# A decoder layer's self-attention: another opening, another written order of steps, another ending

## The chip, the cores and the metric

The kernel runs on one core of a Trainium2 chip. The metric is the device time of one execution in microseconds; lower is better. All numbers are float32.

A core has several engines, each with its own instruction queue that is worked in order: TensorE (PE, matrix multiplications; PEld is its loading of weights), VectorE (DVE), ScalarE (ACT), GpSimd (POOL) and SyncE (SP). SP here issues DMA transfers only. ACT issues a few as well, between its other work. Engines wait for each other by semaphores, so an instruction that waits also holds up everything written behind it on the same engine.

## The reference

A post-norm decoder layer of three parts, with a batch of 2 × 1024 tokens of 256 numbers:

```python
# 1: causal self-attention, 16 heads of 64, rotary positions
q = apply_rope(split_heads(x @ Wq)); k = apply_rope(split_heads(x @ Wk)); v = split_heads(x @ Wv)
sim = jnp.einsum('bid,bjd->bij', q, k) * scale
attn = softmax(where(causal, sim, -inf))
x = layernorm(x + merge_heads(attn @ v) @ Wo + bo)
# 2: cross-attention over 77 context tokens, 16 heads of 64
x = layernorm(x + xattn(x, ctx_1024))
# 3: a router takes the upper half of the tokens by score; they get a GELU network of 1024, the others keep x
x = layernorm(x + where(selected, ffn(x), x))
```

The change touches part 1 alone. Parts 2 and 3 come after it.

## The kernel before

The self-attention part works in 16 *pairs*: 2 batches times 8 pairs of heads (two heads of 64 fill 128 partitions). The class `Pair` holds one pair's tiles. Each pair goes through small *steps*, each named by a letter and up to two digits. The order in which the steps of several pairs are mixed is written by hand in three lists, and the block around them (`tc.manual_schedule()`) keeps it: on each engine instructions stand in the order in which the lists issue them.

- `opening` is a text of steps such as `1Pq0` (pair 1, step `Pq0`), from the first projections until the regular order takes over. `5=` stands for `fill(5)`.
- `steps` is the order inside one *period*, repeated for one pair after another. Each entry has an offset: in the period of pair n, `("w", 1)` is pair n+1's step and `("V0", -1)` that of pair n−1. A step that the opening has done already is passed over.
- `ending` is again a text, from pair 13's last output step on.

The steps, with their engine and the line that does the work:

| step | what it does | engine, line |
|---|---|---|
| Pk0, Pk1, Pq0, Pq1, Pv0, Pv4 | project half of the tokens to k, q or v, into a PSUM bank | PE L268, v L303 |
| Ek0 … Eq1; Ev0, Ev4 | copy that bank out, to `raw`; v to the tile `v` | ACT L276; v L312 |
| d0, d1 | swap the halves of `raw` into `turned`, for the rotation: two DMAs | SP L219 |
| c, s, a | rotate k and q: cosine, sine, sum | POOL L288, L291, L295 |
| w | spread: store the tile `v` to memory (`v_d`), 512 KB | SP L219 |
| l | copies: four DMAs read `v_d` back into `v4`, in four groups of 32 partitions | SP and ACT in turn, L322 |
| S0 … S4 | scores of a group of query tiles | PE L342 |
| T | least of the masked negated scores, by row | DVE L355 |
| X | exponentials, with their sums | ACT L363 |
| R | transpose 32 × 32 blocks of the exponentials | DVE L372 |
| V0 … V7 | output: exponentials times v4; V0 needs all of the pair's R | PE L410 |
| O0 … O3 | copy the output out | ACT L422 |
| Q, I, D, B | sums to a row, inverse, store, and load spread out over partitions (`over`) | PE L380, DVE, SP, SP |
| M, W | scale the output by `over`, store it | POOL L431, SP |
| L | load a pair's weights | SP |
| A, C, Y, Z; f, F, g, z | projection with Wo, sum and norm of one tile of 128 tokens, first and second batch (*closings*): load, project (L473), norm (two steps) | SP, PE, DVE |
| U | copy a closing's projection out of its bank | ACT |
| H, h | turn the second half of batch 0's x by PE, and copy it out | PE L202, ACT |

The tile `v` exists once: Ev0 of the next pair writes into it, and so it waits until the store w has read it. `v4` exists once, too: l waits for the V7 that reads it last. `turned` and `raw` exist twice, and the tiles of exponentials five times. Projections, outputs and a few others share a ring of four PSUM banks; scores have two of their own.

`fill(n)` (L240) runs n matmuls whose result nobody reads; the profile counts each of these as two (x8 for `fill(4)`). `pieces` (L228) says for each pair into how many more matmuls than the least its projections and scores are cut; `split` uses that up from one call to the next. The first DMA begun behind V1 and V7 is tied by `begin` (with `gate`) to those matmuls.

Before the opening the block loads x's first half, pair 0's weights, the rope tables and x's second half on SP, fills, turns the first half of x, fills again, and then follows the three lists.

Of the kernel before, what the change touches and what calls it, by code (L numbers as in the profile page):

```python
# [17 lines left out]
B, T, C = 2, 1024, 256  # L18
H, D = 16, 64
# [15 lines left out]
def decoder_layer(  # L35
# [24 lines left out]
    V, A, G, TE = nc.vector, nc.scalar, nc.gpsimd, nc.tensor  # L60
# [85 lines left out]
    with (  # L146
# [47 lines left out]
        def turn_x(b, first, last, pool=None):  # L194

            for i in range(first, last, 2):
                if i % NH == 0:
                    x_ts[b, i // NH] = e1.tile([P, NC, NB], F32, tag="xT", name=f"xT_{b}", bufs=3)
                pt = ring.tile([P, NC, 2, P], F32, tag="t", name="pt_x")
                for k in range(2):  # L200
                    for c in range(NC):
                        TE.transpose(pt[:, c, k, :], xs[b][:, i + k, c * P : (c + 1) * P], ident)  # L202
                keep = lambda pt=pt, i=i: A.copy(
                    x_ts[b, i // NH][:, :, i % NH * P : (i % NH + 2) * P], pt.rearrange("p c k q -> p c (k q)")
                )
                if b == 0 and i >= NH:
                    kept_later.append(keep)
                elif b == 0 and i == 0:
                    V.tensor_copy(x_ts[0, 0][:, :, : 2 * P], pt.rearrange("p c k q -> p c (k q)"))
                else:  # L210
                    keep()
# [13 lines left out]

        pieces = [0, 1, 13, 13, 11, 10, 11, 12, 13, 12, 8, 9, 8, 8, 9, 0]  # L228
        left = [pieces[0]]

        def split(first, last, most):
# [8 lines left out]
        def fill(n):  # L240

            t = ring.tile([P, NB], F32, tag="t", name="unread")
            for _ in range(n):
                TE.matmul(t, ident, ident.unsqueeze(1).to_broadcast([P, NB // P, P]), start=True, stop=True)  # L244
# [193 lines left out]
        class Closing:  # L438
# [46 lines left out]


        steps = [
            ("Eq0", 1), ("Ek0", 1), ("Ev4", 1), ("Eq1", 1), ("a0", 0), ("R40", -1), ("S0", 0), ("T00", 0), ("T01", 0),
            ("s1", 0), ("V0", -1), ("a1", 0), ("V1", -1), ("d0", 1), ("B", -2), ("S1", 0), ("V2", -1), ("T10", 0),
            ("V3", -1), ("V4", -1), ("T11", 0), ("S2", 0), ("X00", 0), ("V5", -1), ("R00", 0), ("X01", 0), ("R01", 0),  # L490
            ("c0", 1), ("Z", -15), ("X11", 0), ("T20", 0), ("V6", -1), ("T21", 0), ("V7", -1), ("w", 1), ("X10", 0),
            ("X20", 0), ("O1", -1), ("S3", 0), ("R10", 0), ("O0", -1), ("R11", 0), ("Q", -1), ("s0", 1), ("O3", -1),
            ("T31", 0), ("l", 0), ("C", 0), ("O2", -1), ("X31", 0), ("Pk1", 1), ("T30", 0), ("I", -1), ("Pv0", 2),
            ("X30", 0), ("M", -2), ("R20", 0), ("Ek1", 1), ("d1", 1), ("R31", 0), ("Ev0", 2), ("D", -1), ("S4", 0),
            ("R30", 0), ("Pq1", 2), ("L", 3), ("W", -2), ("A", 0), ("c1", 1), ("X21", 0), ("Pq0", 2), ("T41", 0),
            ("Pk0", 2), ("X41", 0), ("T40", 0), ("R21", 0), ("R41", 0), ("X40", 0), ("Pv4", 2),
        ]

        pairs = [Pair(n) for n in range(len(keys))]
# [23 lines left out]


        opening = """
            1L 0Pk0 0Ek0 0Pq0 0Eq0 0H 0h 0Pv0 0Pq1 0c0 0d0 0Pk1 0s0 0a0 0Pv4 0Eq1 0S0 0Ek1 0Ev0 1Pk1 0T00 0d1 0T01 1Pq1
            0c1 0Ev4 0s1 0X01 0X00 1Eq1 1Ek1 1Pv0 0a1 0S1 2L 0R00 0w 0R01 1d1 1Pv4 1c1 1Pq0 0T10 0T11 0S2 1Ev4 0T21 1Ev0
            0X10 1Eq0 1Pk0 1s1 1w 2Pq1 0T20 0R10 0l 1Ek0 1d0 0X11 0S3 2Pk0 0R11 0X21 0X20 0T30 1a1 0T31 0X30 0S4 1c0 3L
            0X31 1s0 0R20 0R30 0R21 1a0 2Eq1 0T41 0T40 2Pv4 2Pv0 0X40 2Ek0 0R31 0R40 2Pq0 2Ev4 5= 0X41 1S0 0R41 1T00
            2Eq0 2Ev0 0V0 0V1 1T01 2d0 0V2 1S1 1T11 0V3 1X00 0V4 0V5 1T10 1S2 1X01 1R00 1X11 0V6 0V7 2w 1X10 1T20 0O0  # L530
            1T21 1S3 1R10 1R01 0O1 1T31 2c0 1l 2Pk1 1X20 1R20 0O3 1T30 0O2 3Pv4 0Q 2Ek1 1S4 1X30 2s0 1X21 3Pq1 2c1 3Ev4
            1R11 3Pv0 2a0 3Pk0 1T41 2d1 1R30 1X31 3Pq0 2S0 1T40 1R21 0I 1X41 1X40 1R31 2s1 1R40 0D 1R41 2T00 3Ek0 3Eq1
            2a1 4L 3Eq0 3Ev0 1V0 1V1 3d0 2T01 2X00 1V2 2S1 1V3 1V4 2T10 2T11 1V5 0B 2R00 2S2 2X01 2T20 2T21 1V6 1V7 3c0
            2X11 2R01
        """


        ending = """
            14X10 12M 14X20 14S3 13O0 15s0 14X21 14R11 14R20 14l 13O1 14T31 14T30 14R21 14X30 14X31 15Pk1 15w 13Q 13I
            14S4 15Ek1 14T40 12W 4C 14T41 14X41 13O2 14R10 15a0 15d1 14R31 13O3 14R30 13D 14X40 15c1 14R40 14R41 15S0 4Y  # L540
            15T00 14V0 15T01 15X00 14V1 14V2 15X01 15s1 15a1 14V3 5A 13B 15R00 15S1 15T10 14V4 6A 15X10 14V5 15T11 15S2
            14V6 14V7 15X11 15R01 15T21 15l 15T20 13M 14O3 15S3 7A 15X20 5C 15X21 15R10 15T30 14O0 15T31 15R11 15X30
            15R21 14O1 15R30 15X31 13W 15S4 15R20 15T41 15T40 14Q 5U 14O2 15X41 14I 15R31 15X40 6C 15Q 2= 14D 15I 15R40
            6U 15R41 15V0 4Z 14B 5Y 15V1 15V2 0f 15V3 14M 1f 7C 15V4 15V5 5Z 6Y 15V6 6Z 15D 2f 15V7 15B 15O1 15O3 7U 0n
            15O2 15O0 0F 1F 2F 3f 1g 3F 2g 3g 7Y 4f 3z 0N 5f 7Z 4F 5F 1z 6f 6F 4g 0g 7f 2z 5g 5z 4z 6g 7F 7g 1N 6z 7z 0z
        """
        closings = [[Closing(b, i) for i in range(NT)] for b in range(B)]
        closing = {
# [6 lines left out]
        def do(n, step):  # L555
            if (n, step) in done or not 0 <= n < (NT if step in closing else len(keys)):
                return
            if step in closing:
                b, act = closing[step]
                act(closings[b][n])  # L560
            elif step == "H":
                turn_x(0, NH, NT)
            elif step == "h":
                for keep in kept_later:
                    keep()
            elif step == "N":
                load_cross(n)
            elif step == "n":
                turn_context()
            else:  # L570
                if n == last and step[0] == "O":
                    pairs[n].gathered_scaled(int(step[1]))
                elif n == 0 and step in ("c0", "s0", "a0"):
                    {"c": pairs[0].cosine, "s": pairs[0].sine, "a": pairs[0].rotated}[step[0]](0, V)
                else:
                    acts[step[0]](pairs[n], step[1:])

                if (n, step) in ((NP - 3, "S4"), (NP, "Pv0")):
                    turn_x(1, *((0, NH) if step == "S4" else (NH, NT)))
                if step == "V7" and n + 1 < len(keys):  # L580
                    left[0] = pieces[n + 1]
                if step == "W":
                    for f in later.get(n, ()):
                        f()
            done.add((n, step))
# [36 lines left out]
        with tc.manual_schedule():  # L622
            halves = x[0].rearrange("(t p) c -> p t c", p=P)
            nc.sync.dma_start(xs[0][:, :NH, :C], halves[:, :NH, :])
            do(0, "L")
            nc.sync.dma_start(cos[:, :NB], rope_cos[:, :NB])
            nc.sync.dma_start(xs[0][:, NH:, :C], halves[:, NH:, :])
            nc.sync.dma_start(sin[:, :NB], rope_sin[:, :NB])
            nc.sync.dma_start(cos[:, NB:], rope_cos[:, NB:])
            nc.sync.dma_start(sin[:, NB:], rope_sin[:, NB:])  # L630
            G.iota(xs[0][:, :, C], [[P, NT]], 0, 1, allow_small_or_imprecise_dtypes=True)
            fill(4)
            turn_x(0, 0, NH)
            fill(1)
            follow(opening)
            for period in range(-8, len(keys)):
                for step, further in steps:
                    if step == "A":
                        if period >= NP + 1:
                            do(period - NP - 1, "A")  # L640
                    elif step == "C":
                        for s in "CY":
                            do(period - NP - 2, s)
                    elif step == "Z":
                        do(period - NP - 3, "Z")
                    else:
                        do(period + further, step)
                    if (last - 2, "V7") in done:
                        break
                else:  # L650
                    continue
                break
            follow(ending)
# [10 lines left out]
    c1 = pool("cross1", 1)  # L664
# [91 lines left out]
    Q = HH // 2  # L756
# [396 lines left out]
```

## Time and profile before

| | us |
|---|---|
| median of three runs | 818.18 (814.99 to 819.43) |
| the profiled execution | 815.8, its span 814.0 |
| PE busy | 788.3 (97%) |
| DVE busy | 580.0 (71%) |
| POOL busy | 367.3 (45%) |
| ACT busy | 355.8 (44%) |
| first output matmuls (V0) of pairs 0, 1, 2, 3 | 55.85, 87.1, 117.3, 146.96 |
| V0 of pairs 9, 10, 11, 12, 13, 14 | 324.97, 358.8, 391.75, 424.33, 456.98, 482.8 |

Times count from the start of the span. In the rows of the profile, the first number is an instruction group's busy time (or its start, in a timeline or a chain), `L410` is a line of the kernel, `po_self<-pT,v` names what is written and what is read, and `x128` counts instructions. `[1.70 <-DVE neg L355]` says that the engine was idle for 1.70 us before the row, and that a result of DVE ended it. `SPq` and `ACTq` are DMAs issued by these engines; the duration of such a row is that of issuing, not of the transfer. `PEclk` is the granted clock of TensorE in tenths of full speed, slice by slice.

### The profile page before, as it was taken

To read this page: it belongs to the slowest core of one execution; us is meant where nothing else is said; L and a number is where in the kernel's file an instruction comes from. 1 tells how busy PE (TensorE), PEld (TensorE's weight loads), DVE (VectorE), ACT (ScalarE), POOL (GpSimd) and SP (SyncE) were. 2 spreads that over 40 slices of the span, in tenths; PEclk is the share of its full clock that TensorE was granted. 3 is DMA by queue.
4 is the path that set the end of the run, shared out by engine and by line. 5 is a ranking of instruction groups with operands and counts; after the bars stand their busy time and mean duration, and the time that the engine had idled before them with its cause. 6 is when DMAs were issued, how large, how long until landed. Compare 5 with 4: busy or idle time off the path is not lost.

```text
span 814.0 us, 26605 instructions
## 1 busy us (share of the span) xinstructions
PE 788.3 (97%) x11436; PEld 624.3 (77%) x11436; DVE 580.0 (71%) x1345; ACT 355.8 (44%) x842; POOL 367.3 (45%) x261
## 2 busy tenths in 40 slices
PE   9999999999999999999999989899999999999996
PEld 5566688888888888788888766688778888887745
DVE  2567779669669768678777797526577788888674
ACT  2555566556556655455554554101343333333130
POOL 1733554554554565375473553213032222262574
PEclk9999999999999999999999999999999999999998
DMA  4545387477477577567376466870450000011121
GB/s 168 181 101 144 106 230 207 155 210 200 144 195 209 163 210 203 168 171 208 123 203 180 136 184 159 236 258 1 160 193 1 1 1 0 1 46 58 55 103 52
DMA packets 65328, 112.32 MB, mean 138 GB/s; under 512 B 6497, under 2 KB 43707, under 8 KB 65211
## 3 DMA queue, kind: packets, MB, share of 16 engines
q1 hardware_dynamic: 59067, 89.64, 37.0%
q10 hardware_dynamic: 4608, 16.78, 7.9%
q0 software_dynamic: 1536, 4.20, 1.4%
q8 instruction: 90, 1.47, 0.8%
q14 instruction: 27, 0.22, 0.1%
HBM read 71.24 MB, written 22.59 MB: 115 GB/s over the span
## 4 chain that ended last, share of the span: by engine, by line
PE 87%; DVE 6%; issue 3%; POOL 3%; DMA 1%; ACT 0%; POOLq 0%; DVEq 0%; ACTq 0%
PE po_self L410 19%; PE ps_scores L342 17%; PE pp_kq L268 14%; PE pp_v L303 7%; PE po_cross L995 6%; PE ps_cross L943 6%; PE po_proj L473 6%; PE pp_h L886 3%; PE po_ffn L897 2%; DVE pT L372 1%; PE pt_p L975 1%; PE unread L244 1%; POOL comp L828 1%; POOL e L964 1%; PE ps_vo L739 1%
## 5 line engine op out<-in xcount | busy, mean ns | idle before, releaser
L363 ACT ACTIVATE p<-p,neg 128x768 f32<-128x768 f32 (+7 forms) x256 | 196.3, 768 | 166.2 <-DVE neg L355 163.9
L355 DVE CUSTOM_DVE_ANT_0 p<-ps_scores,fence 128x512 f32<-128x512 f32 (+7 forms) x256 | 179.6, 751 | 103.1 <-PE ps_scores L342 102.4
L372 DVE STREAM_TRANSPOSE pT<-p 128x512 f32<-128x512 f32 (+7 forms) x256 | 176.2, 740 | 11.5 <-ACT p L363 5.5
L410 PE MATMUL po_self<-pT,v 32*64 32x256 f32 (+6 forms) x7808 | 157.8, 297 | 11.9 <-issue 9.0
L410 PEld LDWEIGHTS po_self<-pT,v 32*64 32x64 f32 x7808 | 136.8, 131 | 37.3 <-issue 25.6
L342 PE MATMUL ps_scores<-kq 64*128 64x256 f32 (+3 forms) x1060 | 147.2, 411 | 0.0
L342 PEld LDWEIGHTS ps_scores<-kq 64*128 64x128 f32 x1060 | 93.2, 187 | 39.2 <-issue 26.5
L291 POOL TENSOR_TENSOR turned<-turned,sin 128x1024 f32<-128x1024 f32 x31 | 73.2, 2362 | 104.3 <-DMA turned<-raw 99.4
L268 PE MATMUL pp_kq<-xT,w_pair 128*128 128x256 f32 (+2 forms) x516 | 118.6, 382 | 0.0
L288 POOL TENSOR_TENSOR kq<-raw,cos 128x1024 f32<-128x1024 f32 x31 | 73.2, 2362 | 77.1 <-ACT raw L276 77.1
L268 PEld LDWEIGHTS pp_kq<-xT,w_pair 128*128 128x128 f32 x516 | 86.9, 191 | 24.1 <-issue 11.6
L964 POOL TENSOR_TENSOR e<-e,inv 128x616 f32<-128x616 f32 x32 | 38.2, 1216 | 113.0 <-DVE inv L963 67.3
L120 POOL TENSOR_TENSOR rs<-ve,neg_half 128x1 f32<-128x1 f32 x48 | 27.2, 570 | 108.6 <-DVE ve L118 107.4
L295 POOL TENSOR_TENSOR kq<-kq,turned 128x1024 f32<-128x1024 f32 x31 | 73.5, 2370 | 1.3
L995 PE MATMUL po_cross<-packed,pT 128*128 128x256 f32 (+1 forms) x320 | 72.5, 380 | 0.1
L943 PE MATMUL ps_cross<-wqk,x1T 128*128 128x308 f32 x256 | 69.2, 423 | 0.0
L995 PEld LDWEIGHTS po_cross<-packed,pT 128*128 128x128 f32 (+1 forms) x320 | 60.1, 190 | 9.4 <-ACT pT L981 0.3
L303 PEld LDWEIGHTS pp_v<-w_pair,xT 128*128 128x128 f32 x512 | 61.2, 192 | 4.0 <-issue 2.5
L303 PE MATMUL pp_v<-w_pair,xT 128*128 128x128 f32 x512 | 62.4, 276 | 0.0
L943 PEld LDWEIGHTS ps_cross<-wqk,x1T 128*128 128x128 f32 x256 | 47.4, 190 | 16.2 <-issue 0.8
L956 ACT ACTIVATE e<-e 128x616 f32<-128x616 f32 x32 | 22.9, 717 | 80.8 <-DVE e L952 80.8
L473 PE MATMUL po_proj<-wo,attnT 128*128 128x256 f32 x224 | 53.4, 391 | 1.2 <-issue 1.0
(128 smaller groups left out, 826.1 us busy)
## 6 DMA issues: line engine op xcount, KB each, us to landing
turned<-raw SPq DMA_DIRECT2D x64, 256.0 KB, 4.4
v<-v_d SPq DMA_DIRECT2D x32, 512.0 KB, 11.6
v<-v_d ACTq DMA_DIRECT2D x32, 512.0 KB, 7.3
v_d<-v SPq DMA_DIRECT2D x16, 512.0 KB, 4.6
over<-inv_d SPq DMA_DIRECT2D x32, 256.0 KB, 4.5
attn_d<-out_pair SPq DMA_DIRECT2D x14, 512.0 KB, 4.4
attnT<-attn_d SPq DMA_DIRECT2D x8, 512.0 KB, 5.2
vo_d<-vo SPq DMA_DIRECT2D x2, 1232.0 KB
```

The lines of the kernel that those rows point to most:

```text
L268: TE.matmul(pp[:, cols], self.w[:, c, "kq".index(of), :], x_ts[self.b, n][:, c, cols], start=(c == 0), stop=(c == NC - 1),)
L288: E.tensor_tensor(self.kq[:, :, n * NB : (n + 1) * NB], self.raw[n], self.twice(cos, n), ALU.mult)
L295: E.tensor_tensor(dst, dst, self.turned[n], ALU.add)
L303: TE.matmul(pv[:, i, :], x_ts[self.b, 2 * n // NT][:, c, toks], self.w[:, c, 2, :], start=(c == 0), stop=(c == NC - 1),)
L342: TE.matmul(self.ps[j][:, cols], self.kq[rows, 1, t * P : (t + 1) * P], self.kq[rows, 0, cols.start - at : cols.stop - at], start=True, st ...
L355: V.tensor_tensor_reduce(p[:, span], self.ps[j][:, span], fence[:, T - (t + 1) * P :], -SCALE, -MASKED, ALU.add, ALU.min, neg[:, i : i + 1],)
L363: A.activation(p[:, span], p[:, span], AF.Exp, bias=neg[:, i : i + 1], scale=-1.0, accum_out=self.sums[:, j, t : t + 1],)
L372: V.transpose(p_t[:, first : first + t * step + 1 : step, :], self.p[g, j][:, span].rearrange("p (n k) -> p n k", k=P),)
L410: ins = TE.matmul(self.po[r][j * D : (j + 1) * D, n:, :], self.v4[rows, NT * k + n, j * D : (j + 1) * D], p_t[rows, first:last:step, k * R ...
L473: TE.matmul(self.po, of, wo[:, c, :], start=(c == 0), stop=(c == NP - 1))
L943: TE.matmul(ps[:, g, : Q * S], self.x_t[:, c, :], wqk[:, c, self.b, h : h + Q, :].rearrange("p h s -> p (h s)"), start=(c == 0), stop=(c = ...
L995: TE.matmul(po, self.p_t[:w, k, :], packed[self.b][:w, k, :], start=(k == 0), stop=(k == NK - 1))
```

## The change

The numbers of fills, the pieces and the written order change; what each step does stays as it is.

- Fills: `fill(4)` in front of the first turning becomes `fill(2)`; the `fill(1)` behind it, `5=` in the opening and `2=` in the ending go.
- Opening: the turning of x's second half and `0Pq1` come ahead of `0Pv0`; `1d1` comes ahead of `0w`, and `1d0` ahead of `0l`; the others are mixed differently.
- Steps: on SP the order within a period was d0, B, w, l, d1, D, L, W, A and becomes B, d0, l, w, d1, W, A, L, D. On PE, V4 moves behind S2, and Pv4 ahead of Pk0. On ACT, l's share of the copies moves behind O1, O2, X20, O3 and O0, and the order of exponentials and copies changes a little, as does DVE's and POOL's.
- Ending: `15w` comes ahead of `14l`; closings and the second batch's loads are mixed differently.

```diff
-        pieces = [0, 1, 13, 13, 11, 10, 11, 12, 13, 12, 8, 9, 8, 8, 9, 0]
+        pieces = [2, 1, 13, 13, 11, 10, 11, 12, 13, 14, 8, 9, 8, 7, 5, 0]
...
         steps = [
-            ("Eq0", 1), ("Ek0", 1), ("Ev4", 1), ("Eq1", 1), ("a0", 0), ("R40", -1), ("S0", 0), ("T00", 0), ("T01", 0),
-            ("s1", 0), ("V0", -1), ("a1", 0), ("V1", -1), ("d0", 1), ("B", -2), ("S1", 0), ("V2", -1), ("T10", 0),
-            ("V3", -1), ("V4", -1), ("T11", 0), ("S2", 0), ("X00", 0), ("V5", -1), ("R00", 0), ("X01", 0), ("R01", 0),
-            ("c0", 1), ("Z", -15), ("X11", 0), ("T20", 0), ("V6", -1), ("T21", 0), ("V7", -1), ("w", 1), ("X10", 0),
-            ("X20", 0), ("O1", -1), ("S3", 0), ("R10", 0), ("O0", -1), ("R11", 0), ("Q", -1), ("s0", 1), ("O3", -1),
-            ("T31", 0), ("l", 0), ("C", 0), ("O2", -1), ("X31", 0), ("Pk1", 1), ("T30", 0), ("I", -1), ("Pv0", 2),
-            ("X30", 0), ("M", -2), ("R20", 0), ("Ek1", 1), ("d1", 1), ("R31", 0), ("Ev0", 2), ("D", -1), ("S4", 0),
-            ("R30", 0), ("Pq1", 2), ("L", 3), ("W", -2), ("A", 0), ("c1", 1), ("X21", 0), ("Pq0", 2), ("T41", 0),
-            ("Pk0", 2), ("X41", 0), ("T40", 0), ("R21", 0), ("R41", 0), ("X40", 0), ("Pv4", 2),
+            ("Eq1", 1), ("a0", 0), ("Eq0", 1), ("Ev4", 1), ("S0", 0), ("R40", -1), ("T00", 0), ("s1", 0), ("V0", -1),
+            ("T01", 0), ("Ek0", 1), ("a1", 0), ("V1", -1), ("S1", 0), ("B", -2), ("V2", -1), ("V3", -1), ("T10", 0),
+            ("T11", 0), ("S2", 0), ("X00", 0), ("R00", 0), ("X01", 0), ("V4", -1), ("X11", 0), ("c0", 1), ("V5", -1),
+            ("Z", -15), ("R01", 0), ("d0", 1), ("X10", 0), ("T20", 0), ("V6", -1), ("T21", 0), ("V7", -1), ("S3", 0),
+            ("R10", 0), ("Q", -1), ("O1", -1), ("R11", 0), ("O2", -1), ("X20", 0), ("O3", -1), ("s0", 1), ("O0", -1),
+            ("T31", 0), ("l", 0), ("X31", 0), ("C", 0), ("Pk1", 1), ("T30", 0), ("w", 1), ("Ek1", 1), ("X30", 0),
+            ("Pv0", 2), ("M", -2), ("Ev0", 2), ("S4", 0), ("d1", 1), ("W", -2), ("I", -1), ("R30", 0), ("R31", 0),
+            ("Pq1", 2), ("A", 0), ("Pq0", 2), ("X21", 0), ("T40", 0), ("T41", 0), ("Pv4", 2), ("L", 3), ("D", -1),
+            ("X40", 0), ("Pk0", 2), ("R21", 0), ("X41", 0), ("R41", 0), ("c1", 1), ("R20", 0),
         ]
...
         opening = """
-            1L 0Pk0 0Ek0 0Pq0 0Eq0 0H 0h 0Pv0 0Pq1 0c0 0d0 0Pk1 0s0 0a0 0Pv4 0Eq1 0S0 0Ek1 0Ev0 1Pk1 0T00 0d1 0T01 1Pq1
-            0c1 0Ev4 0s1 0X01 0X00 1Eq1 1Ek1 1Pv0 0a1 0S1 2L 0R00 0w 0R01 1d1 1Pv4 1c1 1Pq0 0T10 0T11 0S2 1Ev4 0T21 1Ev0
-            0X10 1Eq0 1Pk0 1s1 1w 2Pq1 0T20 0R10 0l 1Ek0 1d0 0X11 0S3 2Pk0 0R11 0X21 0X20 0T30 1a1 0T31 0X30 0S4 1c0 3L
-            0X31 1s0 0R20 0R30 0R21 1a0 2Eq1 0T41 0T40 2Pv4 2Pv0 0X40 2Ek0 0R31 0R40 2Pq0 2Ev4 5= 0X41 1S0 0R41 1T00
+            0Pk0 0Ek0 0Pq0 0Eq0 0H 0h 0Pq1 1L 0c0 0d0 0s0 0a0 0Pv0 0Pk1 0Ev0 0Pv4 0S0 0T01 0Eq1 1Pk1 1Pq1 0Ek1 0T00 1Eq1
+            0Ev4 0X00 0d1 0c1 0s1 0X01 1Ek1 0a1 1d1 0R00 1s1 1Pv0 0w 1Pv4 0R01 1c1 0S1 1Pq0 2L 1Eq0 1Pk0 0T10 0T11 0S2
+            0T21 1Ek0 0X11 0X10 1d0 0l 1Ev4 0T20 2Pq1 0R10 1Ev0 0S3 1w 0X21 0R11 1s0 0T31 1c0 0X20 2Pk0 0T30 0S4 0R20
+            2Ek0 0X30 2Eq1 0X31 0R30 1a1 0T40 0R21 1a0 2Pv4 0T41 3L 2Pv0 0X40 0X41 0R31 0R40 2Ev4 2Pq0 0R41 1S0 2Eq0
...
         ending = """
-            14X10 12M 14X20 14S3 13O0 15s0 14X21 14R11 14R20 14l 13O1 14T31 14T30 14R21 14X30 14X31 15Pk1 15w 13Q 13I
+            14S3 14X10 15s0 12M 15w 14X20 14X21 13O0 14R20 14R21 14T31 14T30 13O1 14l 13Q 15Pk1 14X31 14X30 14S4 13I
...
-            15R21 14O1 15R30 15X31 13W 15S4 15R20 15T41 15T40 14Q 5U 14O2 15X41 14I 15R31 15X40 6C 15Q 2= 14D 15I 15R40
-            6U 15R41 15V0 4Z 14B 5Y 15V1 15V2 0f 15V3 14M 1f 7C 15V4 15V5 5Z 6Y 15V6 6Z 15D 2f 15V7 15B 15O1 15O3 7U 0n
+            15R21 4Z 15R20 15R30 14O1 13W 15X31 15S4 15T41 14Q 15X41 15T40 6C 14I 15X40 15Q 15R31 5U 15R40 15I 14D 14O2
+            15R41 15V0 15V1 5Y 15V2 0f 15V3 7C 6U 1f 14B 15D 7U 15V4 5Z 15V5 14M 6Y 15V6 2f 15V7 15B 15O1 6Z 15O3 0n
...
-            fill(4)
+            fill(2)
             turn_x(0, 0, NH)
-            fill(1)
             follow(opening)
```

## The prediction

> **What bounds the kernel now.** First the page: engine totals and granted clock.
>
> ```profile
> PE 788.3 (97%) x11436; PEld 624.3 (77%) x11436; DVE 580.0 (71%) x1345; ACT 355.8 (44%) x842; POOL 367.3 (45%) x261
> ...
> PEclk9999999999999999999999999999999999999998
> ```
>
> TensorE (PE) is busy 97% of the 814.0 us span at full clock in every slice. Nothing else is near it, so the change can win only where PE stands (25.7 us in all) or runs matmuls nobody reads. It can lose wherever something new makes PE stand. So I read next, for one middle period, the chain of work that ended last.
>
> ```profile
> 295.65 3.42 PE po_self L410 x128
> ...
> 308.65 1.72 PE ps_scores L342 x16
> ...
> 323.23 1.73 PE ps_scores L342 x20
> 324.97 3.43 PE po_self L410 x128
> ```
>
> (Start, duration.) The chain is PE alone from one pair's first output matmuls (V0) to the next pair's. V7, the last, ends 13.0 us after V0. The eight periods from 87.1 to 324.97 take 237.87 us, 29.73 each. The four behind them hold a closing's projection (3.46 us): about 33 each.
>
> What stands close behind PE? The timelines of SP and ACT in that period:
>
> ```profile
> 308.71 0.34 SPq L219 DMA_DIRECT2D v_d<-v  x1
> 309.10 1.51 SPq L322 DMA_DIRECT2D v<-v_d  x2
> 314.30 1.14 SPq L219 DMA_DIRECT2D turned<-raw  x2
> ```
>
> ```profile
> 314.18 0.59 ACT L312 COPY v<-pp_v 128x512 f32<-128x512 f32 x1
> 314.66 0.94 ACT L363 ACTIVATE p<-p,neg 128x768 f32<-128x768 f32 x1
> ...
> 317.39 1.15 ACT L363 ACTIVATE p<-p,neg 128x1024 f32<-128x1024 f32 x1 [1.70 <-DVE neg L355]
> 318.59 1.15 ACT L363 ACTIVATE p<-p,neg 128x1024 f32<-128x1024 f32 x1
> ```
>
> The spread (step w, `v_d<-v`) is issued as V7 ends. Its landing is in the answer on DMA issues around 308.7:
>
> ```profile
> v_d<-v SPq DMA_DIRECT2D x1, 512.0 KB, 5.1
> ```
>
> So it lands at 313.8, and Ev0, which rewrites the single `v` tile, starts at 314.18: 0.4 us of slack. The two big copies v4 behind it take 12.2 us.
>
> **The change, part by part. (1) w behind the copies l, pairs 2 to 9.** SP's order in a period was d0, B, w, l, d1, D, L, W; it becomes B, d0, l, w, d1, W, A, L, D. Only w and l matter. What w costs behind l is shown by before's own ending, where 14l stands ahead of 15w:
>
> ```profile
> 470.34 1.24 SPq L322 DMA_DIRECT2D v<-v_d  x2
> 472.01 0.34 SPq L219 DMA_DIRECT2D v_d<-v  x1
> ```
>
> ```profile
> v_d<-v SPq DMA_DIRECT2D x1, 512.0 KB, 11.9
> ```
>
> There w lands 472.01 + 11.9 − 470.34 = 13.57 us after the first copy's issue. Call this time D. In the changed steps ACT's two copies stand behind O1, O2, X20, O3 and O0, and so start about 2.4 us later than SP's; at best w gains all of that: 11.2. I take the middle, 12.35.
>
> Ev0 now waits for w. Behind it on ACT, which works in order, stand X21, X40, X41; their results go through DVE's R41, R20, R40, and V0 needs all of them. Starts in the ACT lines give the pitch: Ev0 0.48, X21 1.03 (with the read of its sum), X40 1.20, X41 about 1.21. The last three transposes:
>
> ```profile
> 318.41 3.23 DVE L372 STREAM_TRANSPOSE pT<-p 128x768 f32<-128x768 f32 x3
> ```
>
> 0.48 + 1.03 + 1.20 + 1.21 + 3.23 = 7.15, and 0.15 for releases: 7.3. From V0 to the next V0: 13.0 + 0.1 + 12.35 + 7.3 = 32.75, against 29.73. PE, whose next Pk0 also waits for Ev0's bank, stands 3.0 us longer per period. Break-even is D = 8.9.
>
> The standing also costs clock. Around V0 of pair 14, by stretches (length, PE, PEld, DVE, ACT, POOL, clock, DMA share, GB/s):
>
> ```profile
> 480.58:483.99 3.41, 1.87 (x22) 1.20 (x18) 3.41 (x5) 0.82 (x2) 0.00 (x0) 1.00 0.99 362
> 483.99:487.40 3.41, 3.19 (x64) 2.17 (x72) 3.26 (x16) 1.73 (x7) 1.50 (x2) 0.50 0.31 123
> 494.22:497.63 3.41, 2.05 (x99) 1.54 (x87) 3.05 (x11) 2.93 (x8) 0.90 (x1) 1.00 0.78 181
> ```
>
> A stretch with 1.87 us of PE work was followed by one at half clock; one with 2.05 was not followed by a drop. The price is in PE's timeline, pair 14's outputs against pair 15's:
>
> ```profile
> 484.21 7.42 PE L410 MATMUL po_self<-pT,v 32*64 32x256 f32 x250 [0.59 <-DVE y L483]
> ...
> 515.62 5.86 PE L410 MATMUL po_self<-pT,v 32*64 32x256 f32 x248 [0.28 <-DVE pT L372]
> ```
>
> 7.42 − 5.86 = 1.56 us. A gap of 3.0 us leaves some 3.41 us stretch with at most 3.41 − 1.5 = 1.91 of work, even split in the middle. The Trainium skill ("TensorE: Matmul & The Clock Gate", Part 1) drops to half rate only after an idle window of about 3.4 us, so by it a 3.0 us gap is free: period 32.75. By the row it is 34.3. I take the row: this chip dropped on a partly idle stretch. Eight periods: 8 × 34.3 − 237.9 = **+36.5** (by the rule +24).
>
> **(2) The same order in pairs 10 to 13.** PE's own period is 32.6 to 33.8 there, no shorter than 32.75, and the wait is covered by the projection: +1, with 0 and +6 as bounds. The copies of x's second batch, queued on ACT behind the wait, add 0.5. Together **+1.5**.
>
> **(3) Opening.** Before, V0 of pair 0 is at 55.85:
>
> ```profile
> 1.45 6.00 PE L244 MATMUL unread<-ident 128*128 128x512 f32 x8 [1.45 <-POOL ident masks.py:199]
> ...
> 49.75 4.46 PE L244 MATMUL unread<-ident 128*128 128x512 f32 x10
> 54.13 1.78 PE L342 MATMUL ps_scores<-kq 64*128 64x512 f32 x12
> ```
>
> With two fills instead of four, four passes stay of eight: the first took 1.02, the next 0.85 each (half clock), so PE is free at 1.45 + 1.02 + 3 × 0.85 = 5.0; the DMA of x's first half landed at 4.71. The transposes run 5.0 to 6.4; Pk0 starts at 6.9 instead of 9.03. Then H waits for x's second half (10.78) and Pq1 for its copies, which returns about 0.8. From there to S1 POOL's rope bounds (S1 27.73, now about 28.4), so the lead is used up and S4 still ends near 44. But before, PE filled from 49.75 because 1S0 waited for 1a0 (ended 52.94), whose swap was queued behind v's copies (landed 47.4). The changed order has that swap ahead. V0 then follows pair 0's last transpose, 7.1 to 7.8 after S4: about 51. That is −4.9; I take **−4.5**, bounds −7.5 (S4 earlier by its 2 us lead) and 0 (copies v4, now issued at 37, landing late). The Skill (same page, Part 4) says that transposes don't count as PE work for the clock. Then removing fills leaves the stretch 2.7 to 6.1 too idle, and the clock opens at 9.5, +1.3. The row has no such case: fills filled that stretch. I give no charge, as the half before 5.0 is still filled, and keep +1.3 in the range.
>
> **(4) Ending.** 15w goes ahead of 14l, which is the good order, but v4 of pair 14 then lands at about 470.3 + 0.4 + 12.2 = 482.9, where its V0 stands (482.77): even. Without the `2=` fill (1.88 us at 512.18, in a wait that remains) PE stands about 2.7 us before 15V0, and the same half-clock stretch follows: **+1.5**, bounds 0 and +4.
>
> **(5) At nothing.** V4 behind S2 and Pv4 before Pk0 swap places on a PE that has both ready. The pieces' sum goes from 138 to 137: one matmul. SP's d1 lands behind w, about 28 us after V0 (27.6 before); s1 and a1 on POOL (2.4 us each) still end by 33, and S1 wants them at V0' + 3.4, 36. If that cover were gone it would cost its lateness, under 2 us a period. D, L and W have over half a period each. The cross and router stages behind 561 are untouched.
>
> Sum on the profiled span: 814.0 + 36.5 + 1.5 − 4.5 + 1.5 = 849.0. The median of the runs, 818.18, stands 4.2 above that span (the profiled run itself 815.8, so 1.8 of it lies around the span and 2.4 between the runs): **853**.
>
> **The rivals.** *The stall without the clock (R2):* the page's rule holds. 849.0 − 12.5 + 4.2 = 841. For it: 1.87 and 2.05 are close, and pair 14's slow stretch is one case. *The copies worse (R4):* D is 13.6 in every period, and the C periods show it: 8 × 1.25 + 5 more = 868. For it: 13.57 is the only row. *Hidden (R3, the other side):* SP's copies run faster alone and w lands within 8.9 us of the first copy's issue. Then no period grows, the ending has its fill's place covered, and only the opening is left: 814.0 − 4.5 + 4.2 = 813.7, 0.55% faster. For it: w alone needs 5.1 us and ACT's half comes later. Against: the order is one queue's, and every row has w plus copies at 12 us or more. It decides at D = 8.9.
>
> **How the numbers follow.** A measurement of this kernel tells about 0.5%, 4.1 us. Chances: forecast 0.50, R2 0.22, R4 0.15, R3 0.13. R3 lies across the bound: 0.08 faster, 0.05 same. All others are slower: 0.87. Range: low, R2 with D at 11.2 (8 × 31.6 − 237.9 = +15) and the good opening: 814.0 + 15 + 1.5 − 7.5 + 4.2, about 828; high, R4 with the ending at +4 and the opening at −3.5: 872. That leaves R3 and little else out.
>
> **What would show it.** Right: ACT's group `v L312` waits for DMA `v_d<-v`, 6 to 8 us a period; `po_self L410` waits for DVE `pT L372` about 3 us in each of eight periods; V0 to V0 is 34 in pairs 2 to 9 and 33 in 10 to 13; the granted clock is below 9 in slices of the first 40%; V0 of pair 0 is near 51. Wrong: w lands within 9 us of the first copy, or Ev0 finds its tile free, or PE stands under 1.5 us a period (no clock drop).

## The result, and the profile after

The changed kernel takes 872.6 us (median of 4 runs, 864.7 to 873.4) against 818.8 before (814.99 to 821.11): a ratio of 1.064 (95% interval 1.061 to 1.068). The forecast was 853, with a range up to 872. The direction and the place are right. The size is at the upper edge: 54 us more instead of 35, as a time 0.6 us beyond the range's end, as a ratio (1.064 against 872 / 818.18 = 1.066) just within it.

The page of the changed kernel, engine totals and granted clock, and from its groups PE's output matmuls and ACT's copies of v:

```profile
PE 802.7 (92%) x11412; PEld 640.7 (74%) x11412; DVE 581.3 (67%) x1345; ACT 349.6 (40%) x842; POOL 366.7 (42%) x261
...
PEclk9989999999899999999999999999999999999988
...
L410 PE MATMUL po_self<-pT,v 32*64 32x256 f32 (+6 forms) x7808 | 168.2, 305 | 34.3 <-issue 30.2
...
L312 ACT COPY v<-pp_v 128x512 f32<-128x512 f32 x32 | 18.7, 589 | 86.3 <-DMA v_d<-v 81.2
```

The same group of copies before:

```profile
L312 ACT COPY v<-pp_v 128x512 f32<-128x512 f32 x32 | 18.7, 586 | 18.4 <-PE pp_v L303 15.1 <-issue 3.2
```

The span is 871.6 us, 57.6 longer. PE stood 43.2 us longer, and it was busy 14.4 us longer, although 9.6 us of fills are gone: it ran more stretches at half clock (mean granted clock 0.975, before 0.992). The copies of v waited 81.2 us for the DMA that reads their tile, in 12 waits. Before, this group stood 18.4 us in all, and none of it for that DMA.

V0 to V0, before and after, shows where the time came from:

| | before | after | difference | forecast |
|---|---|---|---|---|
| start to V0 of pair 1 (opening) | 87.1 | 91.5 | +4.4 | −4.5 |
| pair 1 to 9, eight periods | 237.8 | 283.9 | +46.1 | +36.5 |
| pair 9 to 13, four with a projection | 132.0 | 137.7 | +5.7 | +1.5 |
| pair 13 to 15 (ending) | 57.6 | 56.5 | −1.1 | +1.5, with the next row |
| from V0 of pair 15 | 299.5 | 302.1 | +2.5 | |

One period of the changed kernel, pair 5 to 6. First SP's timeline, then the DMA answer on the spread, then ACT's timeline:

```profile
249.14 1.04 SPq L322 DMA_DIRECT2D v<-v_d  x2
250.23 0.49 SPq L219 DMA_DIRECT2D v_d<-v  x1
```

```profile
v_d<-v SPq DMA_DIRECT2D x1, 512.0 KB, 12.4
```

```profile
249.28 0.31 ACTq L322 DMA_DIRECT2D v<-v_d  x1
249.39 0.95 ACT L363 ACTIVATE p<-p,neg 128x768 f32<-128x768 f32 x1
...
250.32 0.65 ACT L422 COPY out_pair<-po_self 128x256 f32<-128x256 f32 x2
...
262.67 0.59 ACT L312 COPY v<-pp_v 128x512 f32<-128x512 f32 x1 [6.52 <-DMA v_d<-v]
263.16 0.94 ACT L363 ACTIVATE p<-p,neg 128x768 f32<-128x768 f32 x1
...
264.09 1.14 ACT L363 ACTIVATE p<-p,neg 128x1024 f32<-128x1024 f32 x1
...
265.22 1.14 ACT L363 ACTIVATE p<-p,neg 128x1024 f32<-128x1024 f32 x1
```

V7 ends at 249.11, and V0 of pair 6 starts at 269.81. The spread, which before landed 5.1 us after V7, is issued behind SP's two copies and lands at 262.65. Ev0 starts there, 13.5 us after the first copy. The three exponentials behind it follow without a gap, and then DVE:

```profile
266.48 3.23 DVE L372 STREAM_TRANSPOSE pT<-p 128x1024 f32<-128x1024 f32 x3 [1.28 <-ACT p L363]
```

These are R41, R20 and R40. PE then starts V0 after 2.8 us of standing, besides 0.5 us ahead of Pk0. This is the forecast's chain, link by link.

The opening did not go as forecast. Here is the chain that ended last, up to V0 of pair 0, and one row of ACT:

```profile
35.07 9.70 DMA turned<-raw
...
44.92 2.36 POOL turned L291
47.29 2.30 POOL kq L288
49.59 4.64 POOL kq L295 x2
...
54.27 3.36 PE ps_scores L342 x12
57.63 4.54 PE po_self L410 x113
```

```profile
49.62 0.59 ACT L276 COPY raw<-pp_kq 128x512 f32<-128x512 f32 x1 [6.74 <-POOL kq L288]
```

PE was early up to here: S4 starts at 40.92 (42.09 before). The swap 1d0 was issued at 34.6 instead of 37.5, and its second half landed at 44.8 instead of 47.4. But POOL now does 1c0 and both 1a1 and 1a0 behind 1s0, which waits for that landing. Four instructions of 2.3 to 2.4 us end at 54.2, where two had ended at 52.9. And ACT's 2Eq1 stands 6.74 us, because 1c0 still reads the tile that it writes; pair 0's last exponentials are queued behind it.

### The profile page after: what moved, and what is told of

It is laid out like the page before. It is cut to its first block, busy times and chain, and to the rows that moved or that the text cites. A ratio compares the mean times of both kernels' runs of the same rounds, so it can differ in the third digit from the quotient of the medians.

```text
span 871.6 us, 26584 instructions
## 1 busy us (share of the span) xinstructions
PE 802.7 (92%) x11412; PEld 640.7 (74%) x11412; DVE 581.3 (67%) x1345; ACT 349.6 (40%) x842; POOL 366.7 (42%) x261
## 3 DMA queue, kind: packets, MB, share of 16 engines
q10 hardware_dynamic: 4608, 16.78, 8.8%
## 4 chain that ended last, share of the span: by engine, by line
PE 65%; DMA 14%; ACT 6%; issue 5%; DVE 4%; POOL 4%; SPq 1%; POOLq 0%; ACTq 0%; DVEq 0%
PE po_self L410 17%; PE ps_scores L342 12%; DMA turned<-raw 8%; PE po_cross L994 6%; PE ps_cross L942 6%; PE pp_kq L268 6%; PE po_proj L473 6%; ACT p L363 3%; PE pp_h L885 3%; PE pp_v L303 3%; DMA attn_d<-out_pair 2%; ACT raw L276 2%; PE po_ffn L896 2%; DMA v_d<-v 1%; PE pt_p L974 1%
## 5 line engine op out<-in xcount | busy, mean ns | idle before, releaser
L372 DVE STREAM_TRANSPOSE pT<-p 128x768 f32<-128x768 f32 (+7 forms) x256 | 179.1, 748 | 87.2 <-ACT p L363 81.2
L410 PE MATMUL po_self<-pT,v 32*64 32x256 f32 (+6 forms) x7808 | 168.2, 305 | 34.3 <-issue 30.2
L410 PEld LDWEIGHTS po_self<-pT,v 32*64 32x64 f32 x7808 | 149.2, 135 | 57.3 <-issue 48.9
L342 PE MATMUL ps_scores<-kq 64*128 64x256 f32 (+3 forms) x1052 | 152.8, 418 | 5.1 <-POOL kq L295 5.1
L268 PE MATMUL pp_kq<-xT,w_pair 128*128 128x256 f32 (+2 forms) x520 | 123.1, 385 | 15.1 <-ACT v L312 13.9
L342 PEld LDWEIGHTS ps_scores<-kq 64*128 64x128 f32 x1052 | 99.4, 189 | 46.9 <-issue 28.4
L288 POOL TENSOR_TENSOR kq<-raw,cos 128x1024 f32<-128x1024 f32 x31 | 73.2, 2362 | 73.8 <-ACT raw L276 73.8
L295 POOL TENSOR_TENSOR kq<-kq,turned 128x1024 f32<-128x1024 f32 x31 | 73.2, 2363 | 1.3
L942 PEld LDWEIGHTS ps_cross<-wqk,x1T 128*128 128x128 f32 x256 | 47.4, 190 | 16.2 <-issue 0.7
L312 ACT COPY v<-pp_v 128x512 f32<-128x512 f32 x32 | 18.7, 589 | 86.3 <-DMA v_d<-v 81.2
```

Of the source, the lines that this page charges most:

```text
L268: TE.matmul(pp[:, cols], self.w[:, c, "kq".index(of), :], x_ts[self.b, n][:, c, cols], start=(c == 0), stop=(c == NC - 1),)
L288: E.tensor_tensor(self.kq[:, :, n * NB : (n + 1) * NB], self.raw[n], self.twice(cos, n), ALU.mult)
L295: E.tensor_tensor(dst, dst, self.turned[n], ALU.add)
L342: TE.matmul(self.ps[j][:, cols], self.kq[rows, 1, t * P : (t + 1) * P], self.kq[rows, 0, cols.start - at : cols.stop - at], start=True, st ...
L372: V.transpose(p_t[:, first : first + t * step + 1 : step, :], self.p[g, j][:, span].rearrange("p (n k) -> p n k", k=P),)
L410: ins = TE.matmul(self.po[r][j * D : (j + 1) * D, n:, :], self.v4[rows, NT * k + n, j * D : (j + 1) * D], p_t[rows, first:last:step, k * R ...
```

## The experiments

**1. w in front again.** In the changed kernel:

```diff
-            ("Z", -15), ... ("V7", -1), ("S3", 0),
+            ("Z", -15), ... ("V7", -1), ("w", 1), ("S3", 0),
...
-            ("T31", 0), ... ("T30", 0), ("w", 1), ("Ek1", 1), ("X30", 0),
+            ("T31", 0), ... ("T30", 0), ("Ek1", 1), ("X30", 0),
```

> The changed kernel with one entry of the steps moved: the spread w stands directly behind V7 again, so on SP ahead of the copies l; all else as changed. Theory (w's place behind l makes Ev0 late): the standing in pairs 1 to 9 (+46.1 in the two traces) and in the four periods with a projection (+5.7) goes, V0 to V0 is again 29.5 to 30 in pairs 2 to 9, and the time is 872.6 - 52 = about 820 (817 to 824). Rival (the other moves of the steps carry it: ACT's order, B ahead of d0, Pv4 ahead of Pk0): still above 850.

Measured: 822.4 us, ratio to the kernel before 1.003 (0.999 to 1.008). Pair 1 to 9 took 240.9 us. The group of v's copies, with nothing left of the wait:

```profile
L312 ACT COPY v<-pp_v 128x512 f32<-128x512 f32 x32 | 18.7, 587 | 6.2 <-PE pp_v L303 6.2
```

One entry of a list takes back 50 of the 54 us. The kernel before with the changed opening alone takes 824.3 us (experiment 6), so no cost of the other moves of steps and ending is seen beyond the noise once w is in time.

**2. w behind, alone.** In the kernel before:

```diff
-            ... ("V7", -1), ("w", 1), ("X10", 0),
+            ... ("V7", -1), ("X10", 0),
...
-            ("T31", 0), ("l", 0), ... ("Pk1", 1), ("T30", 0), ("I", -1), ("Pv0", 2),
+            ("T31", 0), ("l", 0), ... ("Pk1", 1), ("T30", 0), ("w", 1), ("I", -1), ("Pv0", 2),
```

> The kernel before with one entry of the steps moved: w goes behind l, to the place between T30 and Ek1 that it has in the changed list; opening, ending, fills and all other steps as before. Theory: nearly the whole loss of the steps by this alone, 818.8 + 46 + 6 = about 870 (860 to 875), w landing 13.5 us after the first copy's issue. Rival (the loss needs the changed order of ACT or SP as well): under 840.

Measured: 845.7 us, ratio 1.028 (1.021 to 1.036). Both expectations missed. From pair 1 to 9 w landed 13.2 to 13.6 us after the first copy, as in the changed kernel, but from Ev0 to V0 it took 5.15 us in place of 7.14. Pair 1 to 9 took 266.0 us (+28), and the four projection periods 133.3 (+1.3). So something else of the changed steps makes the late w dearer, though no cost of it is seen by itself.

**3. The changed kernel with the end of its period put back.**

```diff
-            ... ("w", 1), ("Ek1", 1), ("X30", 0),
+            ... ("w", 1), ("Ek1", 1), ("X30", 0), ("R20", 0),
...
-            ... ("X21", 0), ("T40", 0), ("T41", 0), ("Pv4", 2), ("L", 3), ("D", -1),
-            ("X40", 0), ("Pk0", 2), ("R21", 0), ("X41", 0), ("R41", 0), ("c1", 1), ("R20", 0),
+            ... ("X21", 0), ("T41", 0), ("T40", 0), ("Pv4", 2), ("L", 3), ("D", -1),
+            ("X41", 0), ("Pk0", 2), ("R21", 0), ("X40", 0), ("R41", 0), ("c1", 1),
```

> The changed kernel with w still behind l, and only the end of the period put back into the order of before: R20 directly behind X30, T41 ahead of T40, X41 ahead of X40. Behind the late Ev0 stand then X21, X41, X40 and R40, with R21 and R41 beside them: 5.15 us from Ev0 to V0 as in the run with w alone moved, instead of 7.14. Theory (two parts that multiply: w late, and a longer tail behind it): 2.0 us less in each of the eight periods and about 1.2 less in the four with a projection, so 872.6 - 16 - 5 = about 851 (846 to 856), near the run with w alone moved (845.65). Rival (the rest of that difference comes from clock or from SP's order): above 860.

Measured: 849.3 us, ratio 1.038 (1.034 to 1.042), pair 1 to 9 266.1 us. ACT's and DVE's timelines behind the late Ev0:

```profile
255.87 0.59 ACT L312 COPY v<-pp_v 128x512 f32<-128x512 f32 x1 [6.54 <-DMA v_d<-v]
256.35 0.94 ACT L363 ACTIVATE p<-p,neg 128x768 f32<-128x768 f32 x1
257.28 1.14 ACT L363 ACTIVATE p<-p,neg 128x1024 f32<-128x1024 f32 x1
258.41 1.14 ACT L363 ACTIVATE p<-p,neg 128x1024 f32<-128x1024 f32 x1
```

```profile
258.54 2.38 DVE L372 STREAM_TRANSPOSE pT<-p 128x1024 f32<-128x1024 f32 x2 [0.15 <-ACT p L363]
```

Ev0 is as late as before, but R41 runs beside X40, and only R40 is left behind it: V0 at 261.02, 5.15 us after Ev0. In the changed order R41 waits for the last exponential, and R20, ready long before, stands behind it on DVE: two transposes more in series. This order shows no cost while Ev0 has slack (experiment 1); behind a late Ev0 it is worth 872.6 − 849.3 = 23 us.

**4. All copies l on ACT's queue**, in the changed kernel. This was meant to tell the place in a queue from the load on the transfer engines.

```diff
-                    (nc.scalar, nc.sync)[r % 2].dma_start(
+                    nc.scalar.dma_start(
```

> The changed kernel with all four copies l issued by ACT, none by SP; the list is unchanged, so w is still written behind l, but is the first of SP's queue after V7. Theory A (w is late since it stands behind copies in its own queue): w lands 5 to 7 us after V7, Ev0 finds its tile free, and the time falls to about 822 (816 to 828) as with w written first. Theory B (the copies take the transfer engines, whichever queue they stand in): w lands 10 us or more after V7 and the time stays above 855. In both, v4 lands about 13 us after V7, early enough.

Measured: 826.9 us, ratio 1.013 (1.008 to 1.018): the time that theory A expected. But the run does not tell the theories apart. SP's and ACT's timelines of one period:

```profile
225.68 0.34 SPq L219 DMA_DIRECT2D v_d<-v  x1
230.27 1.12 SPq L219 DMA_DIRECT2D turned<-raw  x2
```

```profile
225.82 0.31 ACTq L322 DMA_DIRECT2D v<-v_d  x1
226.18 1.06 ACTq L322 DMA_DIRECT2D v<-v_d  x1
227.27 1.00 ACTq L322 DMA_DIRECT2D v<-v_d  x2
```

With no copy ahead of it on SP, w was issued 0.14 us before the first copy, and not behind the copies. It landed 4.0 us after its issue (3.9 after the first copy) in the periods where its landing is seen, and v's copies stood for PE only (6.0 us in all). v4 landed about 14.5 us after the first copy, early enough. So w came first both in its queue and in time.

What was issued behind the copies shows the load. The swap d1 (`turned<-raw`) was issued at 230.27, 4.6 us after w, on a queue that held no copy. Issues and landings, as medians in us, come first for d1 here, then for d1 in the changed kernel, where two copies and w stand ahead of it in its own queue (253.73), and then for d0 there, with no copies under way (240.28):

```profile
turned<-raw SPq DMA_DIRECT2D x2, 256.0 KB, 9.8
```

```profile
turned<-raw SPq DMA_DIRECT2D x2, 256.0 KB, 9.5
```

```profile
turned<-raw SPq DMA_DIRECT2D x2, 256.0 KB, 4.7
```

The copies delay d1 by about 5 us, whichever queue they stand in. In the queue rows from 231 to 235 the transfer engines work for q10 alone, which is ACT's (its bytes went from 16.78 to 33.56 MB with this edit):

```profile
q10 hardware_dynamic: 228, 0.85, 103.1%
```

And in this kernel's opening pair 1's w was issued at 38.79, behind two swaps of its own queue and 2.8 us after the last of four copies on ACT's:

```profile
v_d<-v SPq DMA_DIRECT2D x1, 512.0 KB, 10.8
```

The changed kernel's w at that place took 11.4 us. So what is shown is that w has to be issued before the copies. That a queue of its own would help it behind them is not shown, and the load on the engines counts.

**5. Fills in the gap.** In the changed kernel, ahead of V0 of pairs 2 to 9:

```diff
-            ... ("S0", 0), ("R40", -1), ("T00", 0),
+            ... ("S0", 0), ("K", -1), ("R40", -1), ("T00", 0),
...
+            if step == "K":
+                if 2 <= n <= 9:
+                    fill(2)
```

> The changed kernel with two unread matmuls (1.7 us of PE at full clock) put between S0 and V0 in pairs 2 to 9, where PE stands 2.8 us; nothing else changed. Theory (the half-clock stretches come from that standing): the drops at 197, 306 and, if the gap behind Ev0 counts, 224 go, and the time is 872.6 - 4 to 7 = about 867 (863 to 870). Rival (clock drops do not depend on it, or the fills push V0): 872 or more.

Measured: 883.2 us, ratio 1.080 (1.075 to 1.085). Pair 1 to 9 took 279.9 us instead of 283.9: the half-clock stretches at 197 and 306 are gone, that at 220, behind Ev0, is not. That part went as expected. But the four periods with a projection, of which only the first has a fill at its start, took 149.7 instead of 137.7 us: PE stood 1.8 to 2.9 us in each, in V5 to V7, without a wait that the profile shows, and each time a half-clock stretch followed. Every such standing ends soon after instructions for PE have landed (last section); why it is so long in these four periods is not settled.

**6. The changed opening on the kernel before** (opening, two fills, first number of pieces; no other edit).

```diff
-        pieces = [0, 1, 13, ...
+        pieces = [2, 1, 13, ...
...
-            1L 0Pk0 0Ek0 0Pq0 0Eq0 0H 0h 0Pv0 ... 5= 0X41 1S0 ...
+            0Pk0 0Ek0 0Pq0 0Eq0 0H 0h 0Pq1 1L ... 0R41 1S0 2Eq0 ...
...
-            fill(4)
+            fill(2)
             turn_x(0, 0, NH)
-            fill(1)
```

> The kernel before with the changed opening, its two fills and its first number of pieces; steps and ending as before. Theory (the opening itself loses, since on POOL 1c0 and 1a1 stand behind 1s0, which waits for its swap): first outputs of pair 1 at 91.5 instead of 87.1, time 818.8 + 4.4 = about 823 (820 to 826). The forecast's step (opening gains 4.5): about 814. Second rival (the opening's loss in the changed kernel came from the steps behind it): 818 to 819.

Measured: 824.3 us, ratio 1.005 (1.001 to 1.009); V0 of pair 0 at 57.8, of pair 1 at 89.2. The opening loses by itself, +2.1, about half of what the table shows for it. The rest lies between pair 0 and pair 1, where the changed kernel's profile has a half-clock stretch at 74.0 that this run does not have.

**7. The same opening, with POOL's order mended.**

```diff
-            ... 1Pv4 0R01 1c1 0S1 ... 0R11 1s0 0T31 1c0 0X20 ... 0R30 1a1 0T40 0R21 1a0 ...
+            ... 1Pv4 0R01 1c1 1a1 0S1 ... 0R11 1c0 1s0 0T31 0X20 ... 0R30 0T40 0R21 1a0 ...
```

> As the kernel with the changed opening alone, but in the opening 1a1 stands directly behind 1c1 and 1c0 directly ahead of 1s0, so that POOL does both before it waits for the swap 1d0. Theory: 2Eq1 on ACT no longer stands 6.7 us for 1c0, pair 0's last exponentials come at about 44 to 48, 1a0 ends at 49.6, V0 of pair 0 starts at about 51.5, and the time is about 818.8 - 4.5 = 814 (811 to 817). Rival (the swap's landing at 44.8 is itself too late, whatever stands behind it): V0 of pair 0 not before 55, and 818 or more.

Measured: 816.95 us, ratio 0.9958 (0.9917 to 0.9998). POOL and PE:

```profile
39.97 2.36 POOL L288 TENSOR_TENSOR kq<-raw,cos 128x1024 f32<-128x1024 f32 x1
43.69 2.36 POOL L291 TENSOR_TENSOR turned<-turned,sin 128x1024 f32<-128x1024 f32 x1 [1.36 <-DMA turned<-raw]
46.13 2.37 POOL L295 TENSOR_TENSOR kq<-kq,turned 128x1024 f32<-128x1024 f32 x1
```

```profile
49.45 1.78 PE L342 MATMUL ps_scores<-kq 64*128 64x512 f32 x12
51.17 4.80 PE L410 MATMUL po_self<-pT,v 32*64 32x256 f32 x192
```

1c0 runs while POOL would have waited, 1a0 ends at 48.5, and V0 of pair 0 starts at 51.2, where the forecast had it. Of the 4.7 us won, pair 0 to 1 gives 1.3 back: PE stood 1.4 us in V6 and V7 without a wait, and a half-clock stretch followed.

**8. The changed ending on the kernel before** (the whole text `ending`; the diff is that of the change).

> The kernel before with the changed ending alone (w of the last pair ahead of l of the one before, no fill ahead of the last outputs, closings in another mixture). The forecast's step: a half-clock stretch in the last outputs, 819.3 + 1.5 = about 821 (818 to 824), the last pair's first outputs 7.5 us long instead of 5.9. Rival (the earlier w wins more than the fill loses): 817 or less.

Measured: 818.0 us, ratio 1.000 (0.998 to 1.002). The half clock came as forecast (PE's timeline: pair 15's first 256 output matmuls, which before took 7.0 us, from 514.50 to 521.48):

```profile
510.07 10.56 PE L410 MATMUL po_self<-pT,v 32*64 32x256 f32 x256 [1.38 <-ACT y L477]
```

But V0 of pair 13 to V0 of pair 15 took 54.7 us instead of 57.6, which pays for it: neither fits alone.

**9. A faster kernel.** The mended opening with pair 0's small matmuls cut in two stretches:

```diff
-            ... 0V4 1T10 1S2 0V5 1R00 0V6 0V7 ...
+            ... 0V4 0V5 1T10 1S2 1R00 0V6 0V7 ...
```

> The kernel before with the mended opening, and in it 0V5 put ahead of 1T10 and 1S2, as in the opening of before, so that pair 0's small output matmuls stand in two stretches and not in one of V5 to V7. Theory (the long stretch is what PE's 1.4 us of standing without a wait at 65 and the half clock behind it came from): pair 0 to pair 1 takes about 31 us instead of 32.6, and the time is 816.9 - 1.5 = about 815.5, 0.5% under the kernel before (0.3 to 0.8%). Rival (the standing is there wherever the stretch is cut): 817, 0.3% under.

Measured: 812.4 us, ratio 0.993 (0.991 to 0.996). Pair 0 to 1 took 30.4 us, and no half-clock stretch followed. The cut itself is less well shown than the time. With pair 0's long stretch uncut, PE stood 1.3 to 1.7 us in it in all seven traces, and the half clock followed in four of them (the changed kernel, experiments 3, 5 and 7) but not in three (1, 4 and 6). In the five traces with it cut (the kernel before, experiments 2, 8 and both of this one) PE stood 0.9 to 1.7 us, in two parts, and the half clock followed in none. With the changed ending as well:

> The same kernel with the changed ending as well. The ending alone gave a ratio of 1.000, so both theories expect the time of the kernel without it, 815.5 (813 to 818); lower only if the ending's earlier w counts for more behind the shorter opening, which nothing seen so far says.

Measured: 810.3 us, ratio 0.991 (0.987 to 0.994). The two intervals overlap, so what the ending adds is open. Both beat the kernel before and the changed one.

## Why the prediction was right, and where it missed

**(1) w behind l: right in mechanism, short in two terms, long in one.** That w's place is the cause is shown by moving that one entry both ways (experiments 1 and 2). Whether w's queue has a share in it, beside the load of the copies issued before it, is open (experiment 4). The sum said 34.3 us a period; measured 35.5. In the parts of the sum, over eight periods:

- The time D from the first copy to w's landing was taken as 12.35; the trace has 13.65 on average (13.5 to 13.9): +10.4. The step that failed: "ACT's two copies stand behind O1, O2, X20, O3 and O0, and so start about 2.4 us later". They were issued 0.2 and 0.5 us behind V7's end. ACT ran X20 at 249.39 and O3 and O0 at 250.32, after the first copy's issue at 249.28: written ahead of it, they did not hold it back. The measured row, 13.57, should have been taken as it was; the rival R4 did so, and its sum, 868, is the nearest.
- V0 to V7 was taken from one period as 13.0. The mean of the eight periods before is 13.3, and that of the changed kernel 14.2, of which two half-clock stretches are 3.7 us in all: +6.0 beside these.
- The half clock was charged to all eight periods, 12.5 us. It came in three: the outputs of pairs 4 and 7 took 15.4 us to V7 instead of 13.5, and behind Ev0 of the period from pair 4 to 5 it cost 3.2. Together about 7: −5.6.
- The tail from w's landing to V0 was taken as 7.3 and is 7.2 without a half clock: −0.8. From V7's end to the first copy it took 0.03 us and not 0.1: −0.6.

10.4 + 6.0 − 5.6 − 0.8 − 0.6 = 9.4, against the 9.6 by which +46.1 exceeds +36.5. Of the signs named, L312's waits came as said (6.5 to 8.4 us each). PE's standing ahead of V0 was 2.8 us, but its group puts it down to no wait ("issue") and not to DVE; and the clock is below 9 in two of the first sixteen slices, one of them in the opening. The break-even was summed wrongly: 29.73 − 13.0 − 0.1 − 7.3 is 9.3 and not 8.9. At 13.65 nothing turned on it.

The tail had the right size, but the forecast did not see that it was itself a part of the change. "At nothing" named only PE, SP and POOL; DVE's R20 behind R41 and the swapped X40 and X41 were in the tail's 3.23 us of transposes, and experiment 3 prices them at 23 us with w late.

**(2) Periods with a projection:** +5.7, near the forecast's upper bound. The step that failed is "the wait is covered by the projection", by the same D: 13.4 + 13.8 + 7.2 = 34.4 is longer than PE's own 33. With the shorter tail (experiment 2) they were covered: +1.3.

**(3) Opening: wrong.** The failed step is "the changed order has that swap ahead. V0 then follows pair 0's last transpose". The swap was ahead, and its landing at 44.8 was early enough; but what is queued behind the waiting 1s0 on POOL was not looked at. Experiment 7 moves just those two and gets V0 at 51.2.

**(4) Ending:** the half-clock stretch came, its price was paid back by an earlier start; alone the ending is worth 0.0 ± 0.2% instead of +1.5. The two rows of the table make +1.4 together, but that is in part luck: pair 13 to 15 is shorter, and behind it the changed kernel's trace has 6.8 us of half clock at 832, long after the ending, where the trace before has none.

**(5) The clock.** The forecast weighed the row (1.87 us of PE work in a stretch, then half clock) against the Trainium skill's rule of a whole idle window ("TensorE: Matmul & The Clock Gate", Part 1). Neither was enough. Three pairs of neighbouring stretches of the changed kernel, in windows of PE's clock steps, with the columns length, PE, PEld, DVE, ACT, POOL, clock, DMA share, GB/s:

```profile
159.31:162.72 3.41, 1.55 (x51) 1.58 (x59) 3.41 (x9) 1.45 (x4) 3.00 (x2) 1.00 0.02 5
162.72:166.13 3.41, 3.41 (x104) 2.99 (x90) 0.66 (x6) 2.25 (x10) 0.00 (x0) 1.00 0.00 0
...
193.44:196.86 3.42, 1.10 (x33) 1.13 (x41) 3.42 (x10) 1.46 (x3) 3.42 (x2) 1.00 0.00 0
196.86:200.27 3.41, 3.41 (x81) 3.41 (x73) 1.11 (x6) 2.70 (x12) 0.13 (x1) 0.50 0.02 5
```

```profile
70.56:73.97 3.41, 1.93 (x126) 1.77 (x111) 2.26 (x7) 2.39 (x7) 0.00 (x0) 1.00 0.02 5
73.97:77.39 3.42, 3.42 (x16) 2.11 (x13) 0.78 (x1) 2.26 (x7) 0.00 (x0) 0.50 0.74 220
```

1.55 us of work kept the clock, 1.10 and 1.93 us lost it. So no stretch had to be wholly idle, and PE's busy time alone does not decide. PE's work in the first stretch was 51 output matmuls of 256 columns, in the second 33 of the same; in the third it was 122 output matmuls, most of 32 and 64 columns, and at its end four of scores. The groups by shape in the first stretch, then in the third:

```profile
L410 PE MATMUL po_self<-pT,v 32*64 32x256 f32 x51 | 1.9, 380 | 2.8 <-issue 2.8
```

```profile
L410 PE MATMUL po_self<-pT,v 32*64 32x32 f32 x40 | 1.0, 224 | 1.5 <-issue 1.5
L410 PE MATMUL po_self<-pT,v 32*64 32x64 f32 x64 | 1.0, 238 | 0.0
L342 PE MATMUL ps_scores<-kq 64*128 64x256 f32 x4 | 0.9, 510 | 0.0
L410 PE MATMUL po_self<-pT,v 32*64 32x96 f32 x18 | 0.4, 241 | 0.0
```

By the columns that the outputs stream, an estimate from these counts, the first had 51 × 256 = 13,000, the second 8,400 and the third 7,100. That is in the order of what happened, but three stretches make no rule.

Removing the first fills did not hold the clock at half any longer: it opened at 5.7 us in the changed kernel (6.1 before), so the charge for transposes that the forecast kept in its range did not come; fills still filled that stretch up to 5.0, so the rule itself was not put to a test.

## What to carry to other kernels

A DMA that frees a single-buffered tile is to be issued before large transfers; a queue of its own is no substitute that these runs show. Its price is read from any place in the trace where the two already stand in the other order, and that row is to be taken as it is. Before an in-order engine is given a waiting instruction, list what stands behind it, there and on every engine that it feeds (here DVE and POOL). An order that shows no cost while a buffer has slack can nearly double the price of the stall when the slack is gone (here from 27 to 50 us above experiment 1), so such edits have to be costed together.

## What the runs showed of the hardware

- The same 512 KB write landed 4.0 us after its issue when it was issued 0.14 us before four 512 KB reads (experiment 4), and 12.2 to 12.6 us after it when issued behind them (the changed kernel).
- Two 256 KB swaps issued behind such reads took 9.5 us with two of the reads in their own queue and 9.8 us with all of them in another engine's; with none under way 4.7 us. How the transfer engines share their time between two queues is open.
- A copy written behind X20, O3 and O0 on ACT was issued before these three ran (249.28 against 249.39 and 250.32).
- PE's busy time in a stretch of 3.41 us does not tell whether half clock follows: 1.55 us kept the full clock, 1.93 us of smaller matmuls lost it. The exact measure is open.
- PE stood 0.3 to 3.0 us inside long stretches of small matmuls, with no wait in the trace (1.48 us at 73.2 in the changed kernel). In the opening, cutting one stretch in two left 0.6 and 0.35 us in place of 1.44 in one trace, and 1.08 and 0.35 with the changed ending as well; no half clock followed in either.
- Each of these stands (120 of over 0.25 us in the twelve traces) ends 1.2 to 1.6 us after a transfer of the kind "instruction" has landed. For the one above, that transfer ran from 70.83 to 71.77, and PE stood from 71.73 to 73.20. The queue's row from 70.8 to 71.8, and its row for the whole execution:

```profile
q8 instruction: 1, 0.02, 5.9%
```

```profile
q8 instruction: 90, 1.47, 0.7%
```

PE's 11412 matmuls and as many weight loads make about 254 instructions for each of the 90 transfers of 16 KB, and just before this stand PE ran 157 small matmuls with their weight loads in 2.0 us. So PE seems to have run out of instructions there. No run changed that alone.
